# Moving three of eight C products of a selective scan from VectorE to GpSimd

## The chip, the cores and the metric

The kernel runs on one core of a Trainium2 chip. The metric is the device time of one execution in microseconds (us), taken as the median of several runs. A profile of one execution tells what each engine did: TensorE (PE for its products, PEld for its weight loads), VectorE (DVE), ScalarE (ACT), GpSimd (POOL) and the queue of SyncE (SP), which issues the transfers.

## The reference

One sequence of L = 4096 tokens with 1024 features goes through a Mamba layer and a dense layer, all in float32. Cut to what matters:

```python
x = hs; h_in = layernorm(x)
proj = h_in @ in_proj_w                      # 1024 -> 2 * 2048
xc, z = split(proj)                          # 2048 channels each
xc = silu(causal_conv4(xc))
ssm = xc @ x_proj_w.T                        # 64 + 16 + 16 columns: dt, B, C, each rms-normalised
dt = softplus(dt_r @ dt_proj_w.T + dt_bias)
for t in range(L):                           # per channel d and state n (16 states)
    h[d, n] = exp(dt[t, d] * A[d, n]) * h[d, n] + dt[t, d] * B[t, n] * xc[t, d]
    y[t, d] = sum_n h[d, n] * C[t, n]
x = x + ((y + D * xc) * silu(z)) @ out_proj_w.T
out = x + layernorm(x) @ dequantised_W.T + bias   # 1024 x 1024
```

## The kernel before

**Tiling.** Channels lie on the 128 partitions and tokens along the free axis. The scan runs in blocks `(c, s, g)`: eight chunks `c` of 512 tokens, two spans `s` of `TS` = 256 tokens in each, four groups `g` of 512 channels. That gives 64 blocks. Each block has two halves `hf` of 256 channels, and each half has eight units `k`. A unit takes two channel tiles `j` and two of the 16 states `n`, so it is a 128 x 1024 piece of work. There are 64 x 2 x 8 = 1024 units.

**A unit** (`unit`, lines 623 to 650). ScalarE puts the carried state into the first column of a tile `h` (L631). GpSimd fills the rest of `h` with `u * B` (L632), where `u` is `dt * xc`. ScalarE makes `exp(dt * A)` in the PSUM tile `da` with four instructions (L638). VectorE runs the recurrence over the 1024 columns, from `da` and `h` into `da` (L640). It then multiplies `da` by `C` into `h` (L641, "the C product"). ScalarE saves the last column as the new state (L644). TensorE transposes `h` in eight 128 x 128 pieces and adds them up over the states in the PSUM tile `py` (L649). `da` has two buffers in PSUM; `h` comes from the pool `hp`, which has four buffers that are handed out in turn.

**Around the units.** `prep_group` makes `dt`, `u` and the carried term `cy` of the next block, asked for in the third unit of a block (`PREP_N`). `epilogue` takes `py` of a finished half, adds `D * xc` on VectorE (L608), multiplies by `silu(z)` on GpSimd (L609) and stores `y`. `load_bc` loads B and C broadcast over the partitions.

**Background.** All dense products (`gen_x`, `gen_z`, `gen_out`, `gen_ffn`, with the lines L294 to L296 of `product`) come from one generator. After each unit `pull` draws from it until its counted work reaches a share of `total` that grows with the units done, `LAG` = 32 units behind. A chunk's scan needs `("x", c)`, so at the chunk's start the generator is drawn that far whatever the pace. What is left over runs after the scan.

**Order.** Each engine has one queue and takes its instructions in that order, waiting at each for its inputs and its buffer. The order is written when the program is built, by a scheduler that goes by the program's order and by priorities (`tc.high_priority`).

Of the kernel before, what the change touches and what calls it, by code (L numbers as in the profile page):

```python
# [11 lines left out]
F32 = mybir.dt.float32  # L12
# [3 lines left out]
ALU = mybir.AluOpType  # L16
# [4 lines left out]
P = 128  # L21
TC = 512
TS = 256
BIG = 1e28
LAG = 32
# [9 lines left out]
MM = 213.0  # L35
# [4 lines left out]
def mamba_ffn_kernel(ctx, tc, hs, in_w, conv_w, conv_b, xp_w, dt_w, dt_b, a_log, d_par, out_w,  # L40
                     dt_ln, b_ln, c_ln, q_scales, q_vals, f_bias, out):
    nc = tc.nc
    _, L, H = hs.shape
    DIN = conv_w.shape[0]
    N = a_log.shape[1]
# [16 lines left out]
    def pool(name, bufs, **kw):  # L62
        return ctx.enter_context(tc.tile_pool(name=name, bufs=bufs, **kw))
# [7 lines left out]
    cio = pool("cio", 4)  # L71
    dtp = pool("dtp", 2)
    up = pool("up", 2)
    hp = pool("hp", 4)
    bcp = pool("bcp", 8)
    tmp = pool("tmp", 4)
    ldp = pool("ldp", 2)
# [11 lines left out]
    ident = cst.tile([P, P], F32, name="ident")  # L89
# [450 lines left out]
    def prep_group(c, s, g):  # L540

        rr = ctx_c[c]["rr"][:, s * TS:(s + 1) * TS]
        xl = ldp.tile([P, 4, TS], F32, tag="xl", name="xl")
        nc.sync.dma_start(xl, xc_s[c][g][:, :, s * TS:(s + 1) * TS])
        dt = dtp.tile([P, 4, TS], F32, tag="dt", name="dt")
        if (c, s, g) == (0, 0, 0):
            w0 = hp.tile([P, 4, 2, P], F32R, tag="h", name="dtw0")
            nc.sync.dma_start(w0.bitcast(F32), dtw_s[g])
        for k in range(2):
            ps = fgt("dps")  # L550
            for i in range(2):
                j = 2 * k + i
                o = ps[:, i * TS:(i + 1) * TS]
                if (c, s, g) == (0, 0, 0):
                    w = w0[:, j]
                else:
                    w = ldp.tile([P, 2, P], F32R, tag="dtw", name="dtwt", bufs=2)
                    nc.sync.dma_start(w.bitcast(F32), dtw_s[g][:, j])
                nc.tensor.matmul(o, w[:, 0, :], rr, start=True, stop=False)
                nc.tensor.matmul(o, w[0:R, 1, :], rr[0:R], start=False, stop=True)  # L560
            r = tmp.tile([P, TC], F32, tag="tmp", name="r")
            for i in range(2):
                d = g * 4 + 2 * k + i
                o = slice(i * TS, (i + 1) * TS)
                nc.scalar.activation(r[:, o], ps[:, o], AF.Relu, scale=-1.0, bias=capd[:, d:d + 1])
            nc.scalar.activation(r, r, AF.Exp, scale=-1.0, bias=capc)
            l = tmp.tile([P, TC], F32, tag="tmp", name="l")
            nc.scalar.activation(l, r, AF.Ln, bias=lnb)
            q = tmp.tile([P, TC], F32, tag="tmp", name="q")
            nc.scalar.activation(q, r, AF.Square, scale=math.sqrt(0.5))  # L570
            nc.gpsimd.tensor_tensor(r, r, q, ALU.subtract)
            for i in range(2):
                d = g * 4 + 2 * k + i
                o = slice(i * TS, (i + 1) * TS)
                nc.vector.scalar_tensor_tensor(ps[:, o], ps[:, o], dtb[:, d:d + 1], l[:, o], ALU.add, ALU.max)
            nc.vector.tensor_tensor(dt[:, 2 * k:2 * k + 2, :], ps.rearrange("p (a b) -> p a b", b=TS),  # L576
                                    r.rearrange("p (a b) -> p a b", b=TS), ALU.max)
        u = up.tile([P, 4, TS], F32, tag="u", name="u")
        gs = slice(g * 4, g * 4 + 4)
        cy = smp.tile([P, 4, N], F32, tag="cy", name="cy")  # L580
        nc.gpsimd.tensor_tensor(cy, amat[:, gs, :], dt[:, :, 0:1].to_broadcast([P, 4, N]), ALU.mult)
        nc.scalar.activation(cy, cy, AF.Exp)
        b0 = smp.tile([P, N], F32, tag="b0", name="b0")
        nc.sync.dma_start(b0, b0_s[c][s].partition_broadcast(P))
        nc.gpsimd.tensor_tensor(u, dt, xl, ALU.mult)
        nc.gpsimd.memset(dt[:, :, 0:1], BIG)
        ub = smp.tile([P, 4, N], F32, tag="ub", name="ub")
        nc.gpsimd.tensor_tensor(ub, u[:, :, 0:1].to_broadcast([P, 4, N]), b0.unsqueeze(1).to_broadcast([P, 4, N]), ALU.mult)
        nc.gpsimd.tensor_tensor(cy, cy, state[:, gs, :], ALU.mult)
        nc.gpsimd.tensor_tensor(cy, cy, ub, ALU.add)  # L590
        return dt, u, cy

    def epilogue(c, s, g, hf, yt):

        ts_ = slice(s * TS, (s + 1) * TS)
        j0 = 2 * hf
        xl = ldp.tile([P, 2, TS], F32, tag="xe", name="xe", bufs=4)
        nc.sync.dma_start(xl, xc_s[c][g][:, j0:j0 + 2, ts_])
        zl = ldp.tile([P, 2, TS], F32, tag="xe", name="ze", bufs=4)
        nc.sync.dma_start(zl, sz_s[c][g][:, j0:j0 + 2, ts_])  # L600
        ps = dense("yps")
        for j in range(2):
            for tb in range(NTS):
                nc.tensor.transpose(ps[:, j * TS + tb * P:j * TS + (tb + 1) * P], yt[:, tb, j, :], ident)
        for j in range(2):
            d = g * 4 + j0 + j
            o = ps[:, j * TS:(j + 1) * TS]
            nc.vector.scalar_tensor_tensor(xl[:, j, :], xl[:, j, :], dpar[:, d:d + 1], o, ALU.mult, ALU.add)  # L608
        nc.gpsimd.tensor_tensor(xl, xl, zl, ALU.mult)  # L609
        t = starts[c] + s * TS  # L610
        o = max(i for i in range(NOC) if ostarts[i] <= t)
        ts_ = slice(t - ostarts[o], t - ostarts[o] + TS)
        if (c, s, g) == blocks[-1]:
            for j in range(2):
                hi, lo = act_pair("yh", TS)
                nc.scalar.copy(hi, xl[:, j, :])
                nc.vector.tensor_tensor(lo, xl[:, j, :], hi.bitcast(F32), ALU.subtract)
                last_y[o, g, j0 + j] = hi, lo
        else:
            nc.sync.dma_start(y_s[o][g][:, j0:j0 + 2, ts_], xl)  # L620
        if ts_.stop == osizes[o] and hf == 1:
            done_marks.add(("y", o, g))

    def unit(c, s, g, hf, k, dt, u, cy, bt, py):

        h = hp.tile([P, 2, 2, TS], F32, tag="h", name="h")
        bb, cc = bt
        js = slice(2 * hf, 2 * hf + 2)
        ns = slice(2 * k, 2 * k + 2)
        with tc.high_priority(10):  # L630
            nc.scalar.copy(h[:, :, :, 0], cy[:, js, ns].rearrange("p j n -> p n j"))  # L631
        nc.gpsimd.tensor_tensor(h[:, :, :, 1:], u[:, js, 1:].unsqueeze(1).to_broadcast([P, 2, 2, TS - 1]),  # L632
                                bb[:, :, 1:].unsqueeze(2).to_broadcast([P, 2, 2, TS - 1]), ALU.mult)
        da = ps_a.tile([P, 2, 2, TS], F32, tag="da", name="da")
        for n in range(2):
            for j in range(2):
                d = g * 4 + 2 * hf + j
                nc.scalar.activation(da[:, n, j, :], dt[:, 2 * hf + j, :], AF.Exp, scale=amat[:, d, 2 * k + n:2 * k + n + 1])  # L638
        flat = da.rearrange("p n a b -> p (n a b)")
        nc.vector.tensor_tensor_scan(flat, flat, h.rearrange("p n a b -> p (n a b)"), 0.0, ALU.mult, ALU.add)  # L640
        nc.vector.tensor_tensor(h, da, cc.unsqueeze(2).to_broadcast([P, 2, 2, TS]), ALU.mult)  # L641
        if not (c == NCH - 1 and s == sizes[c] // TS - 1):
            g0 = g * 4 + 2 * hf
            nc.scalar.copy(state[:, g0:g0 + 2, ns].rearrange("p j n -> p n j"), da[:, :, :, TS - 1])  # L644
        for n in range(2):
            for tb in range(NTS):
                for j in range(2):
                    i = tb * 2 + j
                    nc.tensor.matmul(py[:, i * P:(i + 1) * P], h[:, n, j, tb * P:(tb + 1) * P], ident, is_transpose=True,  # L649
                                     start=(k == 0 and n == 0 and i == 0), stop=(k == N // 2 - 1 and n == 1), skip_group_check=True)  # L650


# [24 lines left out]
    state = cst.tile([P, ND, N], F32, name="state")  # L677
# [63 lines left out]
    blocks = [(c, s, g) for c in range(NCH) for s in range(sizes[c] // TS) for g in range(NG)]  # L741
    total = 48 * 4 * TP + (L - osizes[-1]) / TC * (24 * (24 * MM) + 16 * 4 * TP + 32 * TP)
    total += (L - sizes[0]) / TC * (16 * 24 * MM + 40 * TP + 64 * MM) + L / TC * 16 * 24 * MM
    bg = gen_all()
    done = 0.0
    over = False
# [24 lines left out]
    kk = 0  # L771
    for i, (c, s, g) in enumerate(blocks):
        dt, u, cy = nxt
        for hf in range(2):
            py = ps_y.tile([P, TC], F32, tag="py", name="py")
            for k in range(N // 2):
# [4 lines left out]
                        epilogue(*pend)  # L781
                    pend = None
                kk += 1
                pull(total * min(max(0, kk - LAG), len(blocks) * N) / (len(blocks) * N))
                if i + 1 < len(blocks):
                    if hf == 0 and k == PREP_N:
                        if blocks[i + 1][1:] == (0, 0):
# [46 lines left out]
```

## Time and profile before

| what | value |
|---|---|
| median of 3 runs | 5294.09 us (5292.4 to 5298.82) |
| the profiled execution, its time / its span | 5296.08 us / 5294.3 us |
| busy PE / PEld | 4346.4 us (82%) / 3604.0 us (68%) |
| busy DVE | 4494.3 us (85%), 4050 instructions |
| busy ACT | 3314.2 us (63%) |
| busy POOL | 3229.3 us (61%), 2111 instructions |
| first and last scan instruction start | 197.1 us and 5060.9 us |
| mean granted TensorE clock | 0.891 |

The span is the time from the first to the last instruction of the profiled execution. Busy times are summed over the whole span, so what an engine could gain has to be read from the stretch in which it is late. A group row reads: line, engine, operation, output<-inputs, shapes, count, then busy us and mean ns of one, then idle time in front of the group and what ended it. A wait row reads: who waited, for whom, us in total, times, longest. A row of windows gives for each stretch the busy us of PE, PEld, DVE, ACT and POOL with instruction counts, the granted clock, the busy share of the transfer engines and GB/s.

### The profile page before, as it was taken

How to read it: one execution, taken by the hardware profiler on the slowest of the kernel's cores; microseconds unless marked ns; L12 is line 12 of the kernel's file. 1: busy time of each engine (PE TensorE's matmuls, PEld its weight loads, DVE VectorE, ACT ScalarE, POOL GpSimd, SP SyncE). 2: the span in 40 equal slices, each digit the busy share in tenths (PEclk: the TensorE clock that was granted, in tenths of full speed). 3: DMA queues.
4: the chain of work that ended last, by engine and by line, in shares of the span. 5: the costliest groups of instructions: out<-in, count | busy, mean ns of one | idle time of the engine just before them, and what ended most of it. 6: DMA issues, size and time to landing. Idle time of an engine off the chain costs nothing. (4 is left out here: it accounts for less than half of the span.)

```text
span 5294.3 us, 71082 instructions
## 1 busy us (share of the span) xinstructions
PE 4346.4 (82%) x22880; PEld 3604.0 (68%) x22880; DVE 4494.3 (85%) x4050; ACT 3314.2 (63%) x8002; POOL 3229.3 (61%) x2111
## 2 busy tenths in 40 slices
PE   7777788588788788888888798888988889888887
PEld 6555666466676567667777677666776667677777
DVE  4799974998998989889989899889999899898931
ACT  4676654666666657666667676666666666666621
POOL 0466542766666666667666686656866577777720
PEclk9777888589898899899999899888999899999999
DMA  9544666155464666557654676546764558667687
GB/s 289 174 149 143 220 222 210 44 171 162 151 192 151 219 222 195 171 171 218 209 189 154 194 223 215 159 149 205 222 220 155 178 182 249 226 217 232 208 279 275
DMA packets 665746, 1034.28 MB, mean 195 GB/s; under 512 B 71904, under 2 KB 480992, under 8 KB 664352
## 3 DMA queue, kind: packets, MB, share of 16 engines
q1 hardware_dynamic: 665376, 1029.74, 60.5%
q8 instruction: 184, 3.01, 0.2%
q14 instruction: 186, 1.52, 0.1%
HBM read 816.95 MB, written 212.60 MB: 194 GB/s over the span
## 5 line engine op out<-in xcount | busy, mean ns | idle before, releaser
L632 POOL TENSOR_TENSOR h<-u,bb 128x1020 f32<-128x1020 f32 x1024 | 2425.6, 2379 | 1025.5 <-PE py L649 543.9
L640 DVE TENSOR_TENSOR_SCAN da<-da,h 128x1024 f32<-128x1024 f32 x1024 | 2340.7, 2288 | 239.7 <-ACT da L638 184.5
L638 ACT ACTIVATE da<-dt,amat 128x256 f32<-128x256 f32 x4096 | 1936.0, 479 | 155.1 <-DVE h L641 77.1
L649 PE MATMUL py<-ident,h 128*128 128x128 f32 x8192 | 1236.3, 301 | 467.2 <-DVE h L641 416.1
L649 PEld LDWEIGHTS py<-ident,h 128*128 128x128 f32 x8192 | 1058.9, 156 | 639.5 <-issue 377.6
L641 DVE TENSOR_TENSOR h<-da,cc 128x1024 f32<-128x1024 f32 x1024 | 1244.7, 1218 | 35.6 <-DVE da L640 0.5
L644 ACT COPY state<-da 128x4 f32<-128x4 f32 x960 | 158.9, 166 | 1039.4 <-DVE h L641 1037.2
L294 PE MATMUL ops<-yh,wt 128*128 128x512 f32 (+1 forms) x1152 | 457.3, 400 | 45.2 <-DMA wt<-wo 15.0
L295 PE MATMUL ops<-yh,wt 128*128 128x512 f32 (+1 forms) x1152 | 442.6, 385 | 0.5 <-POOL yh L473 0.4
L296 PE MATMUL ops<-yh,wt 128*128 128x512 f32 (+1 forms) x1152 | 439.1, 381 | 0.0
L294 PE MATMUL ips<-nh,wt 128*128 128x512 f32 x896 | 384.5, 429 | 30.8 <-DMA wt<-wi 12.6
L294 PE MATMUL zps<-nh,wt 128*128 128x512 f32 x896 | 377.4, 421 | 19.3 <-DVE dt L576 13.0
L295 PE MATMUL ips<-nh,wt 128*128 128x512 f32 x896 | 372.1, 415 | 0.0
L296 PE MATMUL ips<-nh,wt 128*128 128x512 f32 x896 | 368.2, 411 | 0.0
L363 DVE SCALAR_TENSOR_TENSOR pre<-ips,cw,pre 128x511 f32<-128x511 f32 (+2 forms) x384 | 282.3, 735 | 100.7 <-ACT pre L360 77.3
L295 PE MATMUL zps<-nh,wt 128*128 128x512 f32 x896 | 366.8, 409 | 0.0
L296 PE MATMUL zps<-nh,wt 128*128 128x512 f32 x896 | 364.4, 407 | 0.0
L609 POOL TENSOR_TENSOR xe<-xe,ze 128x512 f32<-128x512 f32 x128 | 164.8, 1287 | 215.4 <-DVE xe L608 194.6
L294 PEld LDWEIGHTS ops<-yh,wt 128*128 128x128 f32 x1152 | 227.8, 198 | 87.1 <-ACT yh L472 13.4
L631 ACT COPY h<-cy 128x4 f32<-128x4 f32 x1024 | 194.0, 191 | 135.0 <-PE py L649 132.7
L296 PEld LDWEIGHTS ops<-yh,wt 128*128 128x128 f32 x1152 | 226.8, 197 | 36.9
L295 PEld LDWEIGHTS ops<-yh,wt 128*128 128x128 f32 x1152 | 228.2, 198 | 32.1 <-POOL yh L473 0.9
(140 smaller groups left out, 6586.4 us busy)
## 6 DMA issues: line engine op xcount, KB each, us to landing
wt<-wi SPq DMA_DIRECT2D x448, 512.0 KB
wt<-wo SPq DMA_DIRECT2D x288, 512.0 KB
wt<-wf SPq DMA_DIRECT2D x144, 512.0 KB
wi<-wi SPq DMA_DIRECT2D x64, 512.0 KB
xe<-xc SPq DMA_DIRECT2D x128, 256.0 KB
xl<-xc SPq DMA_DIRECT2D x64, 512.0 KB
ze<-sz SPq DMA_DIRECT2D x128, 256.0 KB
bb<-b SPq DMA_DIRECT2D x128, 256.0 KB
```

The lines of the kernel that those rows point to most:

```text
L294: nc.tensor.matmul(ps, wk[:, 0, k % 4, :], hi, start=(k == 0), stop=False)
L295: nc.tensor.matmul(ps, wk[:, 0, k % 4, :], lo, start=False, stop=False)
L296: nc.tensor.matmul(ps, wk[:, 1, k % 4, :], hi, start=False, stop=(k == KT - 1))
L363: nc.vector.scalar_tensor_tensor(o, ps[:, 0:sz - 3 + k], cw[:, m, k:k + 1], o, ALU.mult, ALU.add)
L609: nc.gpsimd.tensor_tensor(xl, xl, zl, ALU.mult)
L631: nc.scalar.copy(h[:, :, :, 0], cy[:, js, ns].rearrange("p j n -> p n j"))
L632: nc.gpsimd.tensor_tensor(h[:, :, :, 1:], u[:, js, 1:].unsqueeze(1).to_broadcast([P, 2, 2, TS - 1]), bb[:, :, 1:].unsqueeze(2).to_broadcas ...
L638: nc.scalar.activation(da[:, n, j, :], dt[:, 2 * hf + j, :], AF.Exp, scale=amat[:, d, 2 * k + n:2 * k + n + 1])
L640: nc.vector.tensor_tensor_scan(flat, flat, h.rearrange("p n a b -> p (n a b)"), 0.0, ALU.mult, ALU.add)
L641: nc.vector.tensor_tensor(h, da, cc.unsqueeze(2).to_broadcast([P, 2, 2, TS]), ALU.mult)
L644: nc.scalar.copy(state[:, g0:g0 + 2, ns].rearrange("p j n -> p n j"), da[:, :, :, TS - 1])
L649: nc.tensor.matmul(py[:, i * P:(i + 1) * P], h[:, n, j, tb * P:(tb + 1) * P], ident, is_transpose=True, start=(k == 0 and n == 0 and i == ...
```

## The change

In the units with `k % 3 == 1` (k = 1, 4, 7: three of eight) the recurrence writes into `h` in SBUF instead of `da`, the saved state is read from there, and the C product runs on GpSimd into a new tile `hc` of the same pool and tag. The pool has six buffers instead of four. To make room, the `xl` tile of `prep_group` has one buffer instead of two, and `xl`/`zl` of `epilogue` share two instead of four. The pacing counts 24 * 8 more products in `total`, and its share reaches 1 at the last unit, where it was 992/1024.

```diff
-    hp = pool("hp", 4)
+    hp = pool("hp", 6)
...
-        xl = ldp.tile([P, 4, TS], F32, tag="xl", name="xl")
+        xl = ldp.tile([P, 4, TS], F32, tag="xl", name="xl", bufs=1)
...
-        xl = ldp.tile([P, 2, TS], F32, tag="xe", name="xe", bufs=4)
+        xl = ldp.tile([P, 2, TS], F32, tag="xe", name="xe", bufs=2)
...
-        zl = ldp.tile([P, 2, TS], F32, tag="xe", name="ze", bufs=4)
+        zl = ldp.tile([P, 2, TS], F32, tag="xe", name="ze", bufs=2)
...
-        nc.vector.tensor_tensor_scan(flat, flat, h.rearrange("p n a b -> p (n a b)"), 0.0, ALU.mult, ALU.add)
-        nc.vector.tensor_tensor(h, da, cc.unsqueeze(2).to_broadcast([P, 2, 2, TS]), ALU.mult)
+        hflat = h.rearrange("p n a b -> p (n a b)")
+        cb_ = cc.unsqueeze(2).to_broadcast([P, 2, 2, TS])
+        if k % 3 == 1:
+            nc.vector.tensor_tensor_scan(hflat, flat, hflat, 0.0, ALU.mult, ALU.add)
+            last = h[:, :, :, TS - 1]
+            hc = hp.tile([P, 2, 2, TS], F32, tag="h", name="hc")
+            nc.gpsimd.tensor_tensor(hc, h, cb_, ALU.mult)
+        else:
+            nc.vector.tensor_tensor_scan(flat, flat, hflat, 0.0, ALU.mult, ALU.add)
+            last = da[:, :, :, TS - 1]
+            nc.vector.tensor_tensor(h, da, cb_, ALU.mult)
+            hc = h
...
-                    nc.tensor.matmul(py[:, i * P:(i + 1) * P], h[:, n, j, tb * P:(tb + 1) * P], ident, is_transpose=True,
+                    nc.tensor.matmul(py[:, i * P:(i + 1) * P], hc[:, n, j, tb * P:(tb + 1) * P], ident, is_transpose=True,
...
+    total += 24 * 8 * MM
...
-                pull(total * min(max(0, kk - LAG), len(blocks) * N) / (len(blocks) * N))
+                pull(total * max(0, kk - LAG) / (len(blocks) * N - LAG))
```

More of the change, by code (lines that the diff above doesn't have):

```diff
@@ L639, in unit @@
         flat = da.rearrange("p n a b -> p (n a b)")
-        nc.vector.tensor_tensor_scan(flat, flat, h.rearrange("p n a b -> p (n a b)"), 0.0, ALU.mult, ALU.add)
-        nc.vector.tensor_tensor(h, da, cc.unsqueeze(2).to_broadcast([P, 2, 2, TS]), ALU.mult)
+        hflat = h.rearrange("p n a b -> p (n a b)")
[10 more added lines that the diff above has]
+            hc = h
         if not (c == NCH - 1 and s == sizes[c] // TS - 1):
             g0 = g * 4 + 2 * hf
-            nc.scalar.copy(state[:, g0:g0 + 2, ns].rearrange("p j n -> p n j"), da[:, :, :, TS - 1])
+            nc.scalar.copy(state[:, g0:g0 + 2, ns].rearrange("p j n -> p n j"), last)
         for n in range(2):
```

## The prediction

> **What bounds the kernel now.** I read the groups of instructions first, then the waits, then the stretches. The costliest groups on the two engines that the change touches:
>
> ```profile
> L632 POOL TENSOR_TENSOR h<-u,bb 128x1020 f32<-128x1020 f32 x1024 | 2425.6, 2379 | 1025.5 <-PE py L649 543.9
> L640 DVE TENSOR_TENSOR_SCAN da<-da,h 128x1024 f32<-128x1024 f32 x1024 | 2340.7, 2288 | 239.7 <-ACT da L638 184.5
> L641 DVE TENSOR_TENSOR h<-da,cc 128x1024 f32<-128x1024 f32 x1024 | 1244.7, 1218 | 35.6 <-DVE da L640 0.5
> ```
>
> One unit costs VectorE 2.288 + 1.218 = 3.51 us and GpSimd 2.38 us. GpSimd's idle time is mostly waiting for TensorE to free an `h` buffer: it runs ahead of the scan by the pool's four buffers. The scan hardly ever waits for GpSimd, as the answer on L640 shows (what its engine sat idle for: us, times):
>
> ```profile
> its engine sat idle before it (us, times) until:
>   ACT da L638: 184.5, 104
> ...
>   POOL h L632: 11.9, 9
> ```
>
> So VectorE sets the pace. The stretches (PE, PEld, DVE, ACT, POOL busy) show by how much, and where not:
>
> ```profile
> 190.00:790.00 600.00, 438.89 (x2118) 360.68 (x2117) 531.78 (x447) 395.12 (x958) 364.04 (x227) 0.77 0.52 173
> 790.00:890.00 100.00, 93.12 (x450) 78.07 (x449) 34.29 (x65) 39.35 (x46) 10.88 (x23) 0.97 0.64 209
> ...
> 2590.00:3190.00 600.00, 507.58 (x2686) 421.87 (x2685) 545.70 (x480) 405.22 (x991) 406.56 (x265) 0.92 0.60 192
> ...
> 5063.00:5210.00 147.00, 133.75 (x888) 120.03 (x887) 26.93 (x54) 24.72 (x51) 7.75 (x14) 0.99 0.91 307
> 5210.00:5295.00 85.00, 59.17 (x438) 55.30 (x435) 18.61 (x44) 11.67 (x25) 6.03 (x11) 0.86 0.69 236
> ```
>
> VectorE is 91% busy in a typical stretch and GpSimd 68%. At 790 the scan of chunk 1 waits for its own dense products. After 5063 there is no scan, only left-over products.
>
> **The order decides.** The diff suggests that 384 x 1.218 = 468 us leave VectorE for an engine with room. But a queue is taken in order, so I read the GpSimd order of the built changed program. A piece of it (queue place, line, output<-inputs):
>
> ```
> 934 L646 hc_17971<-h_17962,cc
> 935 L632 h_18011<-u,bb
> 936 L632 h_18058<-u,bb
> 937 L609 xe<-xe,ze
> 938 L646 hc_18067<-h_18058,cc
> 939 L632 h_18090<-u,bb
> ```
>
> `hc` of a unit stands behind the `h` of the same unit and before the `h` of the next one, in all 384 cases. The product `hc` must wait for the scan of its unit. GpSimd therefore no longer runs ahead: scan, then `hc`, then the next `h`, then the next scan, one after the other. The two buffers more in `hp` do not help, since what is missing is queue order, not buffers. The trace of before shows what VectorE does when the next `h` is late, in the chain that ended last (start, us, what):
>
> ```profile
> 5019.19 2.36 POOL h L632
> 5021.55 0.02 issue
> 5021.57 2.30 DVE da L640
> ```
>
> The scan starts 0.02 us after `h`.
>
> **The sum for the scan.** Every term is on one path.
> - `hc` plus the next `h`, 384 times. `h` is 2.38 us (L632). `hc` has no row; nearest is L585 (`u`, the same engine and operation, 1024 columns, 2381 ns). Bounds: 1.218 us (VectorE's price for this product, L641) and 2 x 1287 = 2.57 us (L609, 512 columns). I take 2.38. 384 x 4.76 = 1828 us.
> - 1024 scans at 2.288 = 2343 us. No row shows a scan that writes SBUF; bounds are the shortest scan, 2.237 us, and for 384 of them the ratio 856/650 between the L115 subtractions on `wiraw` (856 ns) and on `nps` (650 ns), +280 us in all. I keep 2.288.
> - 640 C products left on VectorE, 628 of them right behind their own scan and so before the next: 640 x 1.218 = 780 us.
> - VectorE's other work. By the built order and the row durations, 517 us of it stand directly behind a scan of k = 1, 4, 7, where VectorE would wait 4.76 us for `h`: 517/384 = 1.3 us each, free but for 13 us in crowded places. The other 508 us lie between scans that follow each other, on the path.
> - GpSimd's other work: 785 us stand between `h` and `hc` of one unit, where GpSimd waits for the scan. Between `hc` and the scan of the next such unit VectorE needs at least 3 x 2.288 + 2 x 1.218 = 9.30 us from the first `h` on, and GpSimd 2 x 2.38 for the other two, so 4.5 us are free (3.4 in the pair 7 to 1) for 2.04 on average; 28 us stick out. 10 us stand between `hc` and `h`.
> - Sum: 1828 + 2343 + 780 + 508 + 13 + 28 + 10 = 5510 us.
> - Between instructions VectorE loses 35 ns (L641: 35.6 us of idle for 1024): 2575 on the path, 90 us. Three hand-overs for each `hc` at 0.02 to 0.1 us: 35 us.
> - Chunk 1's wait stays: 66 us of VectorE idle in 790 to 890 and some behind it; the built order has 480 products left in the last 16 units of chunk 0 instead of 552. I take 60.
> - VectorE's other waits from 1000 to 5060 sum to 325 us (162 of them L640 for `da`); those behind k = 1, 4, 7 vanish in the 4.76 us. 5/8 would be 203, a slower pace gives ScalarE more time: I take 100, with 0 and 203 as ends.
> - Scan: 5510 + 90 + 35 + 60 + 100 = 5795 us, against 4866 before (197.1 to 5063).
>
> **Start, tail, small edits.** The start stays at 197 us. After the last transposes TensorE had 912 products of 256 columns and 192 of 512; by the built order 384 of 256 remain, the last `gen_out` half and the last `gen_ffn`. In the trace that pair ran from 5210 to the end, 84 us. With the last `hc` (in the sum), epilogue and hi/lo split in front, some 11 us (transposes 1.0, copies and L608, L609, L617 at row prices), the tail is 95 us instead of 231. The 136 us saved went into the scan as 104 us of TensorE time (456 products of 512 columns at the 0.2275 us between starts), hidden: TensorE's stream in the scan sums to about 3620 us (10056 products x 0.2275, 8192 transposes x 0.114, some 400 us of others) in 5795. Single `xl` and paired `xe`: their loads now wait on SP for the store of the epilogue before; L600 did so already (97 times, 1.7 us each), with 8 units until the use. Nothing taken; uncovered it would be 128 x 1.7 = 218 us, and bb, cc and weight loads queue behind.
>
> Total 197 + 5795 + 95 = 6087 span, +2 around it as before (5296.08 against 5294.3): **6090 us**. The profiled execution lies 2 us above the median, which I ignore.
>
> **Two rules weighed.** Rows: a `wiraw` subtraction, two SBUF inputs, takes 856 ns, an `nps` one, one input in PSUM, 650. The Trainium skill (SBUF — State Buffer, Who interferes with whom) says that a VectorE instruction with two SBUF inputs contends with a GpSimd one that reads SBUF, and one with a single SBUF input does not. The scan still reads `da` from PSUM, so by the rule it keeps its price; by the subtractions' ratio the sum would be 6370.
>
> Row: from 1000 to 1050 us, with little background, PE was busy 24.64 of 50 us and the clock was 0.51. The Trainium skill (TensorE: Matmul & The Clock Gate, What's actually happening) has the clock drop to half after an idle window of about 3.4 us. It speaks against the change, whose transposes wait longer.
>
> **Rivals.**
> - *GpSimd and VectorE overlap* (other side). If GpSimd had the next `h` tiles done before each `hc`, the busiest engine would bound: GpSimd 3201 + 914 = 4115 us, VectorE 4364 - 468 = 3896 in the scan. At the 91% of today 4115 becomes 4520; 197 + 4520 + 95 = 4810. It decides once one `h` stands ahead of `hc`; the order has none. 4%.
> - *`hc` costs what VectorE pays*: 384 x 1.16 = 446 us less, 5645. L585 speaks against it. 5%.
> - *TensorE becomes the bound*: 3620 us of stream need a mean clock below 3620/5795 = 0.62 to decide; at 0.55 the scan is 6580, the time 6870. The stretch 190 to 790 had 0.77. 5%.
> - *No net change* needs 795 us to vanish from serial terms. 1%.
>
> **How the numbers follow.** Forecast 85%. Its low end has no residual waits, no chunk wait, shortest scans and shortest hand-overs: 6090 - 160 - 52 - 13 = 5865. Its high end has all waits (+103), `hc` at 2.57 (+73) and a quarter of the upper bound of scans that write SBUF (+70): 6335. That leaves out the rivals and the rest of that bound, some 2 in 10. 0.2% is about what a measurement can tell from no change. Faster 0.04, same 0.01, slower 0.95.
>
> **What would show it.** Right: DVE falls to about 4030 busy, 66%; POOL rises to 4140; "DVE scan <- POOL h" appears some 384 times with 384 x (4.76 - 1.35) = about 1300 us; POOL's `hc` waits for the scan; PE's wait for buffers at L632 goes; last scan near 5990, tail near 95. Wrong: scans that wait little for `h`, `hc` rows far from 2.38, or a clock under 0.62.

## The result and the profile after

The changed kernel takes 6013.2 us (median of 4 runs, 6009.36 to 6015.0) against 5296.45 us for the kernel before (median of 4, one more than in the table above): the ratio is 1.1351, 95% interval [1.1331, 1.1371]. The forecast was 6090 us, with a range from 5865 to 6335.

The groups of the changed kernel that answer to L632, L640 and L641 of before (same columns; L643 is the scan into `h`, L648 the scan into `da`, L650 the C product on VectorE, L646 the one on GpSimd):

```profile
L632 POOL TENSOR_TENSOR h<-u,bb 128x1020 f32<-128x1020 f32 x1024 | 2404.4, 2375 | 1.5 <-PE py L659 1.4
L648 DVE TENSOR_TENSOR_SCAN da<-da,h 128x1024 f32<-128x1024 f32 x640 | 1466.8, 2293 | 1100.9 <-POOL h L632 1064.5
...
L646 POOL TENSOR_TENSOR hc<-h,cc 128x1024 f32<-128x1024 f32 x384 | 912.9, 2377 | 1154.5 <-DVE h L643 987.1
...
L643 DVE TENSOR_TENSOR_SCAN h<-da,h 128x1024 f32<-128x1024 f32 x384 | 875.5, 2280 | 78.4 <-ACT da L638 42.4
...
L650 DVE TENSOR_TENSOR h<-da,cc 128x1024 f32<-128x1024 f32 x640 | 780.1, 1219 | 18.3
```

GpSimd no longer waits for buffers (543.9 us before, 1.4 now). It waits 987 us for scans, and the scans wait 1064 us for the `h` that stands behind `hc`: two engines hold each other up in turn. Every price is the one assumed: `hc` 2377 ns, a scan into SBUF 2280 ns.

One such turn, VectorE first and GpSimd below (timeline of the changed kernel; start, us, instruction):

```profile
3307.37 0.55 DVE L391 TENSOR_TENSOR ssm<-xps,ssm 128x384 f32<-128x384 f32 x1
3307.83 2.28 DVE L643 TENSOR_TENSOR_SCAN h<-da,h 128x1024 f32<-128x1024 f32 x1
3310.03 0.66 DVE L510 TENSOR_TENSOR xb<-bkps,xb 128x512 f32<-128x512 f32 x1
...
3315.02 2.30 DVE L648 TENSOR_TENSOR_SCAN da<-da,h 128x1024 f32<-128x1024 f32 x1
```

```profile
3310.26 2.40 POOL L646 TENSOR_TENSOR hc<-h,cc 128x1024 f32<-128x1024 f32 x1 [0.73 <-DVE h L643]
3312.61 6.99 POOL L632 TENSOR_TENSOR h<-u,bb 128x1020 f32<-128x1020 f32 x3
```

The scan of the unit ends at 3310.11, `hc` runs to 3312.66, the next `h` takes 2.33 us more, and the next scan starts at 3315.02, 4.91 us after the scan before it ended. What VectorE does in between is small work.

The stretches after (same columns as before):

```profile
2590.00:3190.00 600.00, 470.02 (x2326) 383.68 (x2326) 429.74 (x363) 338.37 (x842) 442.32 (x257) 0.85 0.53 169
...
5921.00:6013.20 92.20, 62.97 (x448) 57.98 (x446) 18.54 (x44) 11.69 (x25) 8.35 (x12) 0.81 0.63 204
```

No engine is busy for more than 79% of the typical stretch, where VectorE had 91%. The scan runs from 200.6 to 5921.4, so 5721 us instead of 4866; behind it lie 92 us instead of 231.

### The profile page after: what moved, and what is told of

It is laid out like the page before. It is cut to its first block, busy times and chain, and to the rows that moved or that the text cites. A ratio compares the mean times of both kernels' runs of the same rounds, so it can differ in the third digit from the quotient of the medians.

```text
span 6013.2 us, 69199 instructions
## 1 busy us (share of the span) xinstructions
PE 4581.8 (76%) x22880; PEld 3768.1 (63%) x22880; DVE 4112.9 (68%) x3666; ACT 3298.7 (55%) x8004; POOL 4111.4 (68%) x2495
## 5 line engine op out<-in xcount | busy, mean ns | idle before, releaser
L632 POOL TENSOR_TENSOR h<-u,bb 128x1020 f32<-128x1020 f32 x1024 | 2404.4, 2375 | 1.5 <-PE py L659 1.4
L648 DVE TENSOR_TENSOR_SCAN da<-da,h 128x1024 f32<-128x1024 f32 x640 | 1466.8, 2293 | 1100.9 <-POOL h L632 1064.5
L646 POOL TENSOR_TENSOR hc<-h,cc 128x1024 f32<-128x1024 f32 x384 | 912.9, 2377 | 1154.5 <-DVE h L643 987.1
L659 PE MATMUL py<-ident,h 128*128 128x128 f32 x5120 | 817.2, 312 | 561.1 <-DVE h L650 510.8
L659 PEld LDWEIGHTS py<-ident,h 128*128 128x128 f32 x5120 | 685.9, 162 | 684.8 <-issue 503.1
L643 DVE TENSOR_TENSOR_SCAN h<-da,h 128x1024 f32<-128x1024 f32 x384 | 875.5, 2280 | 78.4 <-ACT da L638 42.4
L659 PE MATMUL py<-ident,hc 128*128 128x128 f32 x3072 | 507.7, 319 | 442.2 <-POOL hc L646 441.9
L654 ACT COPY state<-da 128x4 f32<-128x4 f32 x600 | 98.8, 165 | 1296.2 <-DVE h L650 1295.0
L650 DVE TENSOR_TENSOR h<-da,cc 128x1024 f32<-128x1024 f32 x640 | 780.1, 1219 | 18.3
L659 PEld LDWEIGHTS py<-ident,hc 128*128 128x128 f32 x3072 | 423.3, 165 | 522.9 <-POOL hc L646 501.8
L294 PE MATMUL ops<-yh,wt 128*128 128x512 f32 (+1 forms) x1152 | 468.5, 408 | 29.6 <-DMA wt<-wo 13.4
L294 PE MATMUL zps<-nh,wt 128*128 128x512 f32 x896 | 391.8, 437 | 40.9 <-DMA wt<-wi 12.9
L294 PE MATMUL ips<-nh,wt 128*128 128x512 f32 x896 | 389.4, 435 | 17.2 <-DMA wt<-wi 7.7
L294 PEld LDWEIGHTS ops<-yh,wt 128*128 128x128 f32 x1152 | 239.1, 208 | 72.6 <-issue 7.1
```

The costliest lines, as they stand in the source:

```text
L294: nc.tensor.matmul(ps, wk[:, 0, k % 4, :], hi, start=(k == 0), stop=False)
L643: nc.vector.tensor_tensor_scan(hflat, flat, hflat, 0.0, ALU.mult, ALU.add)
L646: nc.gpsimd.tensor_tensor(hc, h, cb_, ALU.mult)
L648: nc.vector.tensor_tensor_scan(flat, flat, hflat, 0.0, ALU.mult, ALU.add)
L650: nc.vector.tensor_tensor(h, da, cb_, ALU.mult)
L659: nc.tensor.matmul(py[:, i * P:(i + 1) * P], hc[:, n, j, tb * P:(tb + 1) * P], ident, is_transpose=True, start=(k == 0 and n == 0 and i == ...
```

## The experiments

The theory: the GpSimd queue holds each `hc` between the `h` of its unit and the next `h`, so scan, `hc` and next `h` follow each other. The rivals: GpSimd is too slow for the product in any order, or the pool has too few buffers. All ratios are to the kernel before, with 95% intervals.

### Mending the order, two ways

First way, `hc` in a tag of its own, in the same SBUF:

```diff
-    hp = pool("hp", 6)
+    hp = pool("hp", 4)
...
-            hc = hp.tile([P, 2, 2, TS], F32, tag="h", name="hc")
+            hc = hp.tile([P, 2, 2, TS], F32, tag="hc", name="hc", bufs=2)
```

> Edit: the changed kernel with hc in a tag of its own (h 4 buffers, hc 2 buffers: the same SBUF as 6 shared ones). In the built GpSimd order 362 of the 384 hc products now stand behind one to three later h tiles (lead 0: 22, 1: 151, 2: 162, 3: 49). Theory (the queue order serialises scan, hc and next h): the 1064 us that scans waited for h go, the busiest engine bounds; GpSimd's 4115 us in the scan at the 91% that VectorE reaches before gives 4520, with 197 in front and 95 behind about 4810 us (4700 to 4950). Rival (GpSimd is simply too slow for the C product, or suffers from VectorE beside it): stays above 5294, near 6013.

Measured: 5246.11 us, ratio 0.9902 [0.9884, 0.992]. The wait of the scan for `h`, 1064.5 us in the changed kernel, is now (us in total, times, longest):

```profile
DVE da L648 <- POOL h L632: 80.6, 43, 6.7
```

Second way, the first two instructions of `unit` (L631, L632) put into `unit_h` and called two units ahead, with the shared pool kept:

```diff
-                unit(c, s, g, hf, k, dt, u, cy, bts[c, s, k], py)
+                me = (i * 2 + hf) * 8 + k
+                while hdone <= min(me + 2, len(blocks) * 16 - 1):
+                    ...
+                    hs_[hdone] = unit_h(*b2, hf2, k2, *((dt, u, cy) if i2 == i else nxt), bts[b2[0], b2[1], k2])
+                    hdone += 1
+                unit(c, s, g, hf, k, dt, u, cy, bts[c, s, k], py, hs_.pop(me))
```

> Edit: the changed kernel, same pool of six shared buffers, but the h tile of a unit is made two units ahead of its scan in program order; in the built GpSimd order 383 of 384 hc products stand behind two later h tiles. Theory (queue order): 4700 to 4900 us, as a lead of two is worth 4.76 us and more than covers one hc; little difference from the version with a tag of its own. Rival (six buffers shared by h and hc are too few whatever the order): above 5294.

Measured: 5234.91 us, ratio 0.9884 [0.9869, 0.9898]. Its groups (the line numbers move: L654 is the scan into `da`, L652 `hc`):

```profile
L632 POOL TENSOR_TENSOR h<-u,bb 128x1020 f32<-128x1020 f32 x1024 | 2423.6, 2382 | 80.0 <-PE py L665 75.7 <-DMA row<-_attn_hidden_states_dram 1.5 <-ACT da L644 1.4
...
L654 DVE TENSOR_TENSOR_SCAN da<-da,h 128x1024 f32<-128x1024 f32 x640 | 1463.9, 2290 | 374.4 <-ACT da L644 170.1 <-ACT h L631 89.0 <-POOL h L632 40.5
L652 POOL TENSOR_TENSOR hc<-h,cc 128x1024 f32<-128x1024 f32 x384 | 916.3, 2386 | 414.5 <-DVE h L649 265.3 <-PE py L665 122.9 <-PE nps L223 6.8
```

The same instructions at the same prices, on the same engines; the wait of the scan for `h` falls from 1064.5 to 40.5 us, and the kernel is 778 us shorter than the changed one. Two quite different edits agree. That shows the order as the cause of the loss. The size I expected was wrong: 5235, not 4810. The smaller `xl` and `xe` pools are in the changed kernel and in every version with moved products; they were not run alone, but SP's wait at L600 for the store hardly changed (167 us before, 142 in the changed kernel, 184 with the lead of two).

A lead of one instead of two (`me + 1`):

> Edit: as the version with a lead of two, but the h tile is made one unit ahead; 383 of 384 hc products stand behind one later h tile. Theory: the next scan starts at once, the one after it waits hc + h = 4.76 us less scan and C product 3.51 us = 1.25 us, and GpSimd's other work between h and hc is no longer free: GpSimd bounds, 4750 to 5050 us, 0 to 150 us above the lead of two.

Measured: 5287.05 us, ratio 0.9988 [0.9976, 1.0]. The step from lead two to one, 52 us, lies within the 0 to 150 expected; the level missed as that of the others did. One `h` in hand already brings 726 of the 778 us.

### Buffers, and fewer products

Four shared buffers instead of six (`pool("hp", 4)`), the order as in the changed kernel:

> Edit: the changed kernel with four buffers in the shared pool instead of six; the GpSimd order has every hc right behind its own h, as in the changed kernel. Theory (order, not buffers): within 1.5% of 6013 (6000 to 6100). Rival (buffers limit): 6200 or more, as four buffers hold under three units.

Measured: 6065.7 us, ratio 1.1465 [1.1434, 1.1495]; 0.9% above the changed kernel, inside the theory's range. The scan still waits 1089.7 us for `h`. So in this order the number of buffers hardly matters.

One unit of eight moved, each `hc` right behind its own `h`, and the same with `h` two units ahead:

```diff
-        if k % 3 == 1:
+        if k == 4:
```

> Edit: the changed kernel with only the units k = 4 moved to GpSimd (one of eight); 128 hc products, each right behind the h of its unit. Theory (each hc costs hc + next h on the path): 128 x 4.76 = 609, 1024 scans 2343, 896 C products 1091, about 850 of VectorE's other work not in the gaps, 310 of small losses: scan 5200, in all about 5500 us (5400 to 5600). Rival (VectorE bound as before, 128 x 1.218 = 156 us less on it and the short tail): about 5000 us.

Measured: 5397.75 us, ratio 1.0198 [1.0175, 1.0221], between the theory's 5500 and the rival's 5000, and 2 us under the theory's range.

> Edit: the version with a lead of two with only k = 4 moved (one of eight). VectorE loses 156 us of 4500. If the queue order alone made the one-of-eight version slow (5398), this one lies at or below the paced kernel without the move, 5209: 5100 to 5210 us. Rival (each moved product costs something whatever the order): above 5230.

Measured: 5217.09 us, ratio 0.9858 [0.9843, 0.9873], 7 us over the range and some 0.2% above the paced kernel without any move (5209, next), so not quite as low as the theory had it. The order alone costs 5398 - 5217 = 181 us for 128 products, 1.41 us each; in the changed kernel 778/384 = 2.03 us each.

### The pacing alone, and without it

The kernel before with only the two pacing lines of the diff:

> Edit: the kernel before with only the pacing of the change (24 * 8 more products in total, share 1 at the last unit); all C products on VectorE, pools as before. Theory: the tail behind the scan falls from 231 to about 95 us and the scan stays at 4866, since TensorE has room for 104 us more: about 5160 us (5140 to 5200). Rival (TensorE's extra products delay the scan as much as they shorten the tail): 5260 to 5300.

Measured: 5209.25 us, ratio 0.9833 [0.9819, 0.9848], faster than both kernels. The last scan starts at 5112.0 and ends at 5114.3; behind it lie 93 us, as expected, but the scan grew by 50 us (4866 to 4916). The 104 us of products were hidden by half only. Some 30 of the 50 us are VectorE's own: it is busy for 4389 us in this scan and for 4359 in that of before, since the moved products bring work for VectorE along. How the rest comes about stays open.

The changed kernel with the old pacing:

> Edit: the changed kernel with the pacing of before. Theory: the scan stays at about 5720 us, the tail grows from 94 to about 230 us: about 6145 us (6110 to 6180). Rival (fewer products in the scan make the scan itself shorter): 6013 or less.

Measured: 6142.72 us, ratio 1.1598 [1.1579, 1.1618]. Here the scan had room for the products: the pacing is worth 130 us, and the scan (198.8 to 5912) is as long as in the changed kernel.

### The product from SBUF, on VectorE

```diff
-            nc.gpsimd.tensor_tensor(hc, h, cb_, ALU.mult)
+            nc.vector.tensor_tensor(hc, h, cb_, ALU.mult)
```

> Edit: the changed kernel with hc computed by VectorE instead of GpSimd, all else the same (scan into SBUF, hc in the shared pool); both inputs of this product then lie in SBUF. Theory (queue order): GpSimd runs ahead again, the scan waits little for h; at 1.218 us for hc the scan is 4866 and the time about 5160, at the ratio 856/650 of the two-input subtractions about 5310. If such a product waits for whole GpSimd instructions, as the Trainium skill's SBUF page (Who interferes with whom) would have it, some 1.2 to 2.4 us more for each of 384: 5600 to 6000.

Measured: 5462.43 us, ratio 1.032 [1.0295, 1.0345]. The answers on the two lines in this run (duration ns min/median/max):

```profile
L646 DVE TENSOR_TENSOR hc<-h,cc x384: 1167/1594/5636, 208.9 to 5370.0; 128x1024 f32<-128x1024 f32 x192
```

```profile
L632 POOL TENSOR_TENSOR h<-u,bb x1024: 2325/2382/3465, 198.2 to 5353.9; 128x1020 f32<-128x1020 f32 x171
```

With both inputs in SBUF the product has a mean of 1931 ns (741.6 us for 384) against 1218 ns with `da` in PSUM, and the GpSimd `h` a mean of 2522 instead of 2379 ns. The shortest product, 1167 ns, shows that it isn't the reads themselves. The Trainium skill (SBUF — State Buffer, Who interferes with whom) has a VectorE instruction with two SBUF inputs contend with a GpSimd one that reads SBUF: the one that starts second is blocked until the first has ended. This run agrees. In its trace 125 of the 384 products begin with GpSimd idle and take 1.22 us in the mean; the other 259 begin while a GpSimd instruction runs, take 2.27 us in the mean, and 253 of them end 1.05 to 1.15 us after that instruction does. The mean loss of 0.71 us stayed under the 1.2 to 2.4 us that I had worked out from the page, since a third of the products met no GpSimd instruction at their start and the others waited only for the rest of one. It takes nothing from the theory: even so this version is 551 us faster than the changed kernel, since GpSimd runs ahead again.

### What holds the mended version at 5235

Paced without any move 5209, with a lead of two and three of eight moved 5235: 384 C products less on VectorE (its busy time fell from 4501 to 4100 us) bought nothing. The stretch 2590 to 3190 in the version with a lead of two:

```profile
2590.00:3190.00 600.00, 511.43 (x2725) 426.73 (x2725) 494.36 (x427) 398.42 (x986) 511.98 (x307) 0.92 0.61 194
```

PE, DVE and POOL stand at 82 to 85% each. I asked whether TensorE is the bound, or waits between the other engines. TensorE lightened:

```diff
             nc.tensor.matmul(ps, wk[:, 0, k % 4, :], hi, start=(k == 0), stop=False)
-            nc.tensor.matmul(ps, wk[:, 0, k % 4, :], lo, start=False, stop=False)
             nc.tensor.matmul(ps, wk[:, 1, k % 4, :], hi, start=False, stop=(k == KT - 1))
```

> Edit: the version with a lead of two, leaving out the second of the three products of each dense step (high weights by low activations), so TensorE has some 770 us less to stream; pacing and all else the same. Theory A (once the queue order is mended, TensorE is what keeps the scan at about 4940 us): the time falls to 4750 to 4950 us. Rival B (waits between ScalarE, VectorE and GpSimd inside the units bound it, TensorE does not): within 1.5% of 5235.

Measured: 5112.31 us, ratio 0.966 [0.9645, 0.9674].

> Edit: the kernel before with the new pacing only, leaving out the second of the three products of each dense step, as the control. Theory: VectorE bounds the scan there (4500 us of work), so little is gained but the 50 us by which the extra products lengthened the scan and some of the wait at chunk 1: 5080 to 5170 us, against 5209. If TensorE bounded there too, it would fall below 5000.

Measured: 5129.6 us, ratio 0.9685 [0.9664, 0.9705], as expected of the control.

ScalarE relieved of the saved state:

```diff
-        if not (c == NCH - 1 and s == sizes[c] // TS - 1):
+        if False:
```

> Edit: the version with a lead of two, leaving out the copy of the last column into the saved state (every span then starts from zero state). ScalarE waits 1065 us in all at this copy for VectorE, with the next units' exponentials queued behind it. Theory B (ScalarE's queue, held at this copy, makes the scan wait for da): 4950 to 5100 us. Theory A (TensorE): above 5180, as it only takes 160 us off ScalarE.

Measured: 5105.46 us, ratio 0.9652 [0.9634, 0.967].

Neither A nor B holds as put. A third fewer dense products gave 123 us (2.3%), which is not the 285 to 485 of A and a little more than B allows. The control without moved products gained 80 us by the same edit, so only some 40 of the 123 us go with the move; and with TensorE so lightened the move is worth 17 us (5112 against 5130), which the intervals do not tell from nothing. No state copy gave 130 us, which rules out A's "above 5180" and lies 5 us outside B's range. The waits of the last version suggest why not more (waited, for whom: us in total, times, longest):

```profile
ACT da L644 <- DVE h L656: 787.4, 429, 9.9
ACT da L644 <- DVE h L649: 335.6, 267, 10.5
```

The exponentials now wait themselves where the copy waited (756.8 and 307.8 us with the copy). They need the PSUM buffer `da`, of which there are two. Whether a third `da` would free the scan wasn't tried. So what bounds the mended version stays open: no single removal gave more than 2.5%, with three engines at four fifths in the typical stretch.

## Why the prediction was right

**The mechanism.** The step that decided, read from the built order, held: POOL's wait at L632 for buffers fell to 1.4 us, `hc` waits for L643, L648 waits for L632. The prediction's 384 waits of some 1300 us in all were 305 of 1064 us, in the waits of the changed kernel (us in total, times, longest):

```profile
DVE da L648 <- POOL h L632: 1064.5, 305, 10.2
POOL hc L646 <- DVE h L643: 987.1, 286, 12.8
```

In the gaps behind those scans VectorE is idle for 1516 us, more than the 1300 forecast, but 428 us of that stand before its other instructions, which wait for ScalarE, TensorE and transfers. Of the signs that I had named, VectorE's busy time missed: 4113 us, not 4030. Its rows overlap by 198 us in all against 252 before, and some of its smaller rows took longer.

**The terms.** From the changed kernel's trace, 383 gaps from the end of a moved unit's scan to the next scan:
- They last 2038 us in all, with a median of 4.89 us each. Predicted were 1828 for `hc` and `h`, 51 for what sticks out and 35 for hand-overs, 1914. The rows of `hc` and `h` in them are 1819, as assumed. The mis-sized term is what stands around these rows, 219 us against 86: 77 from the scan's end to the start of `hc` and 156 from the end of `h` to the next scan, less 14 of overlap. In 65 of the gaps, up to 13.1 us long, VectorE is not free when `h` is done: 93 us of other work, for which 13 were allowed, and 52 us of waits for other engines.
- All the rest of the scan is 3683 us. Predicted were 2343 + 780 + 508 + 90 + 60 + 100 = 3881. This is the second mis-sized term, by 198 us. VectorE is busy 3484 us there, 147 us less than its rows sum to (2343 + 780 + 508), and idle 199 us, against 250 for the losses, the wait at chunk 1 and the other waits.
- Between instructions I added 90 us, but the rows of VectorE there add up to more than its busy time. The 35 ns of L641 holds where the second instruction needs the first. Where it doesn't, VectorE's rows overlap: in the timeline above the scan starts at 3307.83, while the row before it (L391, 3307.37 for 0.55 us) ends at 3307.92.
- Chunk 1 still waits: in 850 to 1000 us VectorE is idle for 75 us, but waits for `h` are among them, so the 60 assumed is not measured by itself.
- Tail 92 us against 95, start 200.6 against 197.

The two misses, +124 and -198, make 74 of the 77 us between 6090 and 6013. They are of opposite sign, so that the total came nearer than its two parts is luck.

**The rivals.** "GpSimd and VectorE overlap" was priced at 4810. The run in which they do overlap gave 5235: the condition was right (one `h` ahead of `hc`), the price not. I let the busiest engine reach 91% as VectorE does in the kernel before; here three engines stand at 82 to 85%, and what holds them there stays open. "`hc` costs what VectorE pays" falls by the row, 2377 ns. "TensorE becomes the bound" needed a clock under 0.62; it was 0.83, down from 0.891.

**The two rules.** The scan kept its price with a single SBUF input, 2280 ns, so the sum by the ratio 856/650 (6370) falls. That ratio was no price of two SBUF inputs to begin with. The means mix shapes and a few long instructions; by the medians in the trace of before the two subtractions cost the same (duration ns min/median/max):

```profile
L115 DVE TENSOR_TENSOR nh<-nps,nh x136: 415/679/693, 26.9 to 5261.9; 128x512 fp32r<-128x512 f32 x120, 128x256 fp32r<-128x256 f32 x16
L115 DVE TENSOR_TENSOR wi<-wiraw,wi x64: 673/683/2854, 15.0 to 424.8; 128x512 fp32r<-128x512 f32 x64
```

The clock did fall as TensorE waited more, from 0.92 to 0.85 in 2590 to 3190, without deciding: TensorE was busy for 470 of these 600 us, and the scans waited for `h`.

**The pacing.** The 104 us of products hid in the changed kernel, whose scan is long (6142.72 against 6013.2 without); beside the scan of before half of them showed. The cover that I named is there only as long as the scan leaves TensorE room.

## What to carry to other kernels

Before moving work to an engine with room, read the order of its queue: an instruction that waits for a late result also holds up the early ones behind it that the late result's producer needs. Give the moved result buffers of its own or issue the feeder a step or two ahead; here that was worth 778 us, which is more than the whole loss. And ask what the relieved engine waits for next: with three engines at four fifths, 384 products less on VectorE bought nothing, and moving left-over work under the scan was the only part of the change that paid.

## What the runs showed of the hardware

- Where neighbouring rows overlap in the traces of before and after, VectorE's do so by 83 ns and GpSimd's by 42 ns (medians); a C product, which needs the scan right before it, starts 35 ns after the scan's end.
- With a third fewer dense products the granted clock was lower: 0.828 against 0.891 with the lead of two, 0.816 against 0.897 in the control. The products left took longer: those of L294 for `zps` 443 against 430 ns with the lead of two, and 446 against 426 in the control.
- A VectorE product with two SBUF inputs beside busy GpSimd had 1167 ns at best, 1594 in the median and 5636 at worst. Begun while a GpSimd instruction ran, it ended some 1.1 us after that one's end (253 of 259).
